# A three-layer graph network on one core: banks for the search of places, the place of its preparation, and the pacing of the first layer's seam

## The chip, the core and the metric

One of the eight cores of a Trainium2 chip runs the whole program. The metric is the device time of one execution in microseconds (us); the kernel before takes 2237.45 us, the median of three runs (2230.03 to 2240.05). The engines named below are PE (TensorE matmuls; PEld is its load of weights), DVE (VectorE), ACT (ScalarE), POOL (GpSimd) and SP (SyncE, used here only to issue transfers). PSUM is the memory that PE sums into; it has 8 banks of 512 fp32 per partition.

## The reference

A graph of 6,250 nodes and 100,000 edges, sorted by the node that they end in, goes through three layers. A layer multiplies the node rows by a weight matrix, adds the rows of the neighbours (with loops, both ends scaled by 1/sqrt(degree)), adds a bias and takes the positive part. The result is added to the input, and each row is normalised.

```python
loops = jnp.arange(n); src = concat([src, loops]); dst = concat([dst, loops])
deg = segment_sum(ones, dst, n); dinv = rsqrt(deg)
norm_edge = dinv[src] * dinv[dst]
h = x                                   # 6250 x 256
for W, b in ((W1, b1), (W2, b2), (W3, b3)):   # 256x512, 512x512, 512x256
    h = relu(segment_sum((h @ W)[src] * norm_edge[:, None], dst, n) + b)
x = layernorm(x + h)                    # rows of 256, eps 1e-5
```

## The kernel before

**Tiling.** Nodes are cut into 50 blocks of 125 (Q), degrees and loads into groups of 10 blocks (GRP). The sums over edges of a block are formed in one of two ways. A *gathered* block fetches the rows of its edges from a table in DRAM: POOL issues one indirect transfer of 128 rows at a time (L1365 in the first layer, L1561 in the others), and PE adds the rows to their nodes by a matmul with a one-hot matrix that DVE makes by comparing (L1321). A *dense* block multiplies a 125 by 6,250 matrix of edge counts with all node rows, which lie in SBUF in `parts` (L1450): 50 matmuls, one for each block of sources. These count matrices are themselves made in the first layer by `counts`: DVE compares (L1032) make one-hot matrices, PE multiplies them (L1105), ACT copies the counts out as uint8 (L1066), and SP stores them to `kept` in DRAM.

**Stages.** The *opening* loads the edges (L766, on the queues of SP, ACT and POOL), makes constants (`numbers`, `finder_numbers`), and runs five groups of degree stages (`counted`, from L829): counts of edges per node, 1/sqrt(degree), scaled rows to the first table, and at the end the node rows split into `parts` (`in_parts`, L891 on ACT and L892 on DVE). Then the *first layer* runs (`first_layer`, L1274): 466 gathers for blocks 21 to 49, while blocks 0 to 20 (FEW) are dense. The *second layer* (`layer(1, ...)`) has 599 gathers of 512-wide rows, the *third* (`layer(2, ...)`) 317 gathers and 32 dense blocks with `after3`, which ends in the normalised rows.

**What sets the order.** The whole program is recorded in one fixed order by generators that hand over to each other (`manual_schedule`): the layer's loop takes one gather after another, and with each gather every helper takes a step or counts down its pause (`yield 3` is three gathers). Each engine executes its own instructions strictly in the order recorded. So a number in a helper moves instructions of all engines against each other. The helpers that matter here:

- The **search of places** (`found_rounds` L588, `found_beyond` L628, called by `all_found` L674) works out for 34 blocks, two at a time, which edges the second and third layers gather in which round; its results are `round_src` and `over_src`. It sums into `spot[0]`, which in the first layer is the upper half of the bank `near` (L1008). The lower 250 columns of `near` hold the numbered columns that every DVE compare of L1032 and L1321 reads; a profile's tile name `near_cols` is this bank. `rows_risen` (L567) prepares the search; it runs in the opening's loop, once per group from group 10 on (L932 to L935), summing into `mat_bank`.
- **Banks.** Seven banks circulate in a queue, `common`. A dense sum, a gathered sum, a pair of counts each take one (`one_of_common`) and put it back. `counts` takes one only while more than SPARE stay behind.
- **`teams`** (L1138): four groups of four blocks of the second layer are dense, 800 steps of two matmuls (L1195) over the first layer's result, into four fixed banks. They can start when all counts are stored, the search is done and the result's first rows are back in `parts`. `first_layer` runs some of these steps at its end, the second layer FRONT of them (L1607) before its first product, and `team_goal` (L1899) spreads the rest evenly so that they end TEAMS_END gathers before the last gather.
- **`caching`** (L1123): when all 21 dense blocks of the first layer have ended, SP loads the first layer's result from its table into `parts`, two blocks every three gathers.
- Blocks 26 to TAIL_FROM-1 of the first layer gather 2 KB rows that are already split into two parts; blocks from TAIL_FROM on gather 1 KB rows, which ACT (L1417) and DVE (L1420) split.

Of the kernel before, what the change touches and what calls it, by code (L numbers as in the profile page):

```python
# [23 lines left out]
P = 128  # L24
# [19 lines left out]
SPARE = 1  # L44
# [7 lines left out]
TAIL_FROM = 47  # L52
# [3 lines left out]
FRONT = 24  # L56
TEAMS_END = 70
# [345 lines left out]
def sorted_path(ctx: ExitStack, tc: tile.TileContext, x, edges, starts, found, wts, biases, room, late, out):  # L403
# [105 lines left out]
    spot = [mat_bank[:, :256]]  # L509
    finder_room = room[:, room.shape[1] - 4 * C - 584:room.shape[1] - 4 * C]  # L510
    out_of = finder_room[:, :CHOSEN * WAYS].rearrange("p (c w) -> p c w", w=WAYS)
    hit, value = [finder_room[:, 252 + n * CHOSEN * KF:][:, :CHOSEN * KF].rearrange("p (c j) -> p c j", j=KF) for n in range(2)]
    run = finder_room[:Q, 476:476 + 4 * KF].rearrange("p (b j) -> p b j", b=2)
# [53 lines left out]
    def rows_risen(g, ed, spare):  # L567

        b0 = max(g, FIRST_EDGES)
        size = g + GRP - b0  # L570
        of = slice(b0 - FIRST_EDGES, g + GRP - FIRST_EDGES)
        bits = spare[:, :size * KF].bitcast(BF16).rearrange("p (b k j) -> p b k j", k=2, j=KF)
        for k in range(2):
            number = spare[:, (k + 1) * 2 * P:][:, :size * KF].bitcast(I32).rearrange("p (b j) -> p b j", j=KF)
            nc.vector.tensor_single_scalar(number, ed[:, b0:g + GRP, :, 0], (6, 63)[k], op=(ALU.logical_shift_right, ALU.bitwise_and)[k])
            nc.scalar.copy(bits[:, :, k], number)
        yield
        half = -(-size // 2)
        for n in range(2):
            for b, e in ((0, half), (half, size)):  # L580
                risen = spot[0][:, :(e - b) * 2 * KF]
                nc.tensor.matmul(risen, lhsT=row_steps[n], rhs=bits[:, b:e].rearrange("p b k j -> p (b k j)"), start=True, stop=True)
                yield
                for k in range(2):
                    nc.scalar.activation(rises[:, of, k, 1 + n * KF:1 + (n + 1) * KF][:, b:e],
                                         risen.rearrange("p (b k j) -> p b k j", k=2, j=KF)[:, :, k], AF.Copy, scale=0.5)

    def found_rounds(e):  # L588

        two, bank = range(e, e + 2), spot[0]  # L590
# [7 lines left out]
        yield  # L598
# [5 lines left out]
        yield  # L604
        got = finder.tile([Q, 2, 2, 2 * KF + 1], F32, name="egot")
        nc.scalar.copy(got.rearrange("p b k j -> p (b k j)"), bank[:Q, :2 * each])
        yield
# [18 lines left out]
        yield  # L626

    def found_beyond(e):  # L628

        two, bank = range(e, e + 2), spot[0]  # L630
# [3 lines left out]
        yield  # L634
        for n, m in zip(two, marks):
            for at in (slice(0, 2 * P), slice(2 * P, LANES)):
                wide = at.stop - at.start
                nc.tensor.matmul(bank[:, :wide], lhsT=low_of[:, n, 0:1].to_broadcast([P, P]), rhs=m[:, at], start=True, stop=True)  # L638
                yield
                nc.scalar.activation(past[:, n - e, at], bank[:, :wide], AF.Sign, bias=less16)  # L640
                yield
# [11 lines left out]
        yield  # L653
        nc.scalar.copy(out_of, ways)
        yield
# [14 lines left out]
        yield  # L670
# [3 lines left out]
    def all_found():  # L674

        ahead = 1
# [76 lines left out]
    with tc.tile_pool(name="sdeg1", bufs=1) as dp1, tc.tile_pool(name="sdeg", bufs=2) as dp, \  # L753
# [3 lines left out]
        row_steps = [dp1.tile([P, P], BF16, name=f"esteps{n}") for n in range(2)]  # L757
# [136 lines left out]
        with tc.manual_schedule():  # L894
# [7 lines left out]
            numbers()  # L902
            load_edges(POOL, nc.gpsimd, range(8, GRP))
# [10 lines left out]
            steps_of_numbers = finder_numbers(find_space)  # L914
# [11 lines left out]
            for k in range(NG + 2):  # L926
# [20 lines left out]
            for g in range(2 * GRP, NB, GRP):  # L947
                in_parts(g)
# [174 lines left out]
    def caching():  # L1123

        while finished < FEW:
            yield 1
# [989 lines left out]
```

## Time and profile before

| what | us |
|---|---|
| median of three runs (lowest, highest) | 2237.45 (2230.03, 2240.05) |
| the profiled execution, whole | 2235.24 |
| its span, from first to last instruction | 2233.4 |
| first gather issued | 102.7 |

A profile shows one execution. "Busy" is the time in which an engine executes; a row of groups gives the line, the engine, output and input tiles, the count, the busy time with the mean ns of one, then the engine's idle time just before these instructions and what ended most of it. A row of waits reads: engine, tile and line that waited, then the engine, tile and line waited for, and the total us, the number of waits, the longest. A row of windows gives the busy time of every engine in a stretch with its number of instructions, the granted TensorE clock (1.00 is full), the mean busy share of the 16 DMA engines (over 1 where rows overlap) and GB/s.

### The profile page before, as it was taken

What the parts mean: (1) busy time and instruction counts of PE and PEld (TensorE: products, weight loads), DVE (VectorE), ACT (ScalarE), POOL (GpSimd) and SP (SyncE); (2) the same over time, 40 slices, a digit from 0 to 9 for tenths busy, and PEclk for the clock granted to TensorE, in tenths of its full rate; (3) what the DMA queues carried; (4) which work ended last, traced back from release to release, by engine and by line L of the source; (5) the groups of instructions that cost most, each with busy time, mean ns of one, the idle gap of its engine ahead of it and who ended that gap; (6) DMA issues with size and microseconds to landing.
All of it is one profiled execution on the core that took longest, in us unless ns stands there. A gap on an engine that the chain in (4) does not pass through costs nothing. (4 is left out here: it accounts for less than half of the span.)

```text
span 2233.4 us, 29538 instructions
## 1 busy us (share of the span) xinstructions
PE 1887.6 (85%) x8654; PEld 1433.4 (64%) x8654; DVE 1583.6 (71%) x3141; ACT 1121.3 (50%) x2183; POOL 1434.9 (64%) x1426
## 2 busy tenths in 40 slices
PE   2468988788889965968999899899976889999996
PEld 1356666555666633646787687688765666777775
DVE  5576677677767773577777777767767468888876
ACT  0546566566667643633444444445433345555552
POOL 2145555455557655577777777777776477777775
PEclk9989999999999966979999999999988899999998
DMA  6566477677679999477777777777788567777784
GB/s 145 156 200 191 134 202 179 169 184 189 180 201 256 250 300 233 137 235 208 218 221 224 210 220 222 213 217 220 217 244 227 152 172 202 201 203 206 204 213 128
DMA packets 227394, 451.33 MB, mean 202 GB/s; under 512 B 44147, under 2 KB 103234, under 8 KB 227220
## 3 DMA queue, kind: packets, MB, share of 16 engines
q0 software_dynamic: 119376, 305.25, 50.1%
q1 hardware_dynamic: 92004, 132.23, 21.3%
q10 hardware_dynamic: 15840, 11.86, 2.1%
q8 instruction: 70, 1.15, 0.2%
q14 instruction: 104, 0.85, 0.1%
HBM read 376.81 MB, written 69.81 MB: 200 GB/s over the span
## 5 line engine op out<-in xcount | busy, mean ns | idle before, releaser
L1561 POOL DMA_INDIRECT room<-tab,round_src x728 | 765.8, 1052 | 265.9 <-issue 132.8
L1621 DVE TENSOR_TENSOR total<-total,room 125x512 f32<-125x512 f32 (+1 forms) x694 | 410.6, 592 | 82.8 <-DMA room<-tab,round_src 72.0
L1365 POOL DMA_INDIRECT halves<-both,efirst_src x318 | 300.5, 945 | 240.7 <-PE sacc L1399 59.6
L1032 DVE TENSOR_TENSOR room<-near_cols,slots 128x625 bf16<-128x625 f32 (+2 forms) x390 | 300.2, 806 | 119.8 <-PE near_cols L638 31.9
L1162 ACT CAST dense_rows<-parts 125x512 fp32r<-125x512 f32 x200 | 123.9, 619 | 270.6 <-PE smm L1195 268.6
L1164 DVE TENSOR_TENSOR dense_rows<-parts,dense_rows 125x512 fp32r<-125x512 f32 x200 | 137.9, 689 | 133.8 <-ACT dense_rows L1162 131.5
L1561 POOL DMA_INDIRECT room<-tab,over_src x182 | 189.0, 1038 | 64.5 <-issue 34.1
L1271 ACT CAST piece<-room 125x625 fp32r<-125x625 uint8 x217 | 151.8, 713 | 106.3 <-PE win_ps L1644 35.1
L1365 POOL DMA_INDIRECT room<-tab,efirst_src x128 | 128.4, 1003 | 102.6 <-PE smm L1399 31.0
L1577 PE MATMUL sacc<-halves,shot 128*125 128x512 f32 x430 | 144.3, 437 | 51.4 <-ACT halves L1613 36.5
L1195 PE MATMUL sacc<-dense_rows 125*125 125x512 f32 x400 | 140.9, 427 | 43.1 <-DVE dense_rows L1164 16.8
L1613 ACT CAST halves<-room 128x512 fp32r<-128x512 f32 (+1 forms) x188 | 101.0, 544 | 148.6 <-DMA room<-tab,over_src 87.4
L1616 DVE TENSOR_TENSOR halves<-room,halves 128x512 fp32r<-128x512 f32 (+1 forms) x188 | 110.6, 598 | 62.7 <-ACT halves L1613 60.3
L1271 ACT CAST dense_rows<-room 125x625 fp32r<-125x625 uint8 x210 | 149.3, 724 | 6.6 <-PE smm L1450 1.9
L1105 PEld LDWEIGHTS <-room 128*125 128x125 bf16 x650 | 90.1, 147 | 87.3 <-issue 65.0
L1577 PEld LDWEIGHTS sacc<-halves,shot 128*125 128x125 f32 x430 | 86.5, 203 | 87.0 <-ACT halves L1613 41.9
L1644 PE MATMUL win_ps<-parts,piece 125*125 125x512 f32 x550 | 139.5, 405 | 0.0
L1195 PE MATMUL mat_ps<-dense_rows 125*125 125x512 f32 x400 | 136.4, 423 | 0.5 <-DVE room L1740 0.5
L1195 PE MATMUL smm<-dense_rows 125*125 125x512 f32 x400 | 135.2, 419 | 1.1 <-DVE room L1740 1.1
L1644 PE MATMUL smm<-parts,piece 125*125 125x512 f32 x505 | 128.4, 407 | 8.1 <-DVE piece L1271 8.1
L1195 PE MATMUL near_cols<-dense_rows 125*125 125x512 f32 x400 | 133.8, 416 | 0.0
L1321 DVE TENSOR_TENSOR shot<-near_cols,edlo 128x500 fp32r<-128x500 f32 x110 | 74.0, 673 | 77.5 <-PE sacc L1399 29.4
(460 smaller groups left out, 4326.5 us busy)
## 6 DMA issues: line engine op xcount, KB each, us to landing
kept<-room SPq DMA_DIRECT2D x32, 683.6 KB
room<-kept SPq DMA_DIRECT2D x32, 683.6 KB
tab<-st SPq DMA_DIRECT2D x58, 224.0 KB
parts<-tab SPq DMA_DIRECT2D x28, 448.0 KB
room<-tab,round_src POOLq DMA_INDIRECT x728, 3.9
both<-parts SPq DMA_DIRECT2D x10, 1120.0 KB
room<-kept SPq DMA_DIRECT2D x160, 68.4 KB
room<-in_x SPq DMA_DIRECT2D x50, 112.0 KB
```

What stands on the lines that cost most here:

```text
L1032: nc.vector.tensor_tensor(out, numbered[0][:, :shape[2]].unsqueeze(1).to_broadcast(shape), numbers.unsqueeze(2).to_broadcast(shape), op=AL ...
L1162: nc.scalar.copy(to[:, :HID], row)
L1164: nc.vector.tensor_sub(to[:, HID:], row, to[:, :HID].bitcast(F32))
L1195: nc.tensor.matmul(team_banks[n][:Q], lhsT=team_pieces[u % 2][:, n, :], rhs=both_parts[u % 2][:, h * HID:(h + 1) * HID], start=(u % NB == ...
L1271: convert(piece, matrix[:, c * PIECE:(c + 1) * PIECE, :])
L1365: nc.gpsimd.indirect_dma_start(out=row, out_offset=None, in_=table, in_offset=bass.IndirectOffsetOnAxis(ap=at, axis=0))
L1561: nc.gpsimd.indirect_dma_start(out=row, out_offset=None, in_=tables[i], in_offset=bass.IndirectOffsetOnAxis(ap=at, axis=0))
L1577: nc.tensor.matmul(acc[:Q, :size], lhsT=hots[b][:, k], rhs=two[:, c0:c0 + size], start=(k == c0 == 0), stop=(k == BEYOND + 1 and c0 + size ...
L1613: nc.scalar.copy(two[:, :width], landed[chunk - hi_lag])
L1616: nc.vector.tensor_sub(two[:, width:], landed.pop(chunk - lo_lag), two[:, :width].bitcast(F32))
L1621: nc.vector.tensor_add(own, parts[:, b].bitcast(F32) if i == 1 and r == 0 else own, landed.pop(chunk - ADDED[i])[:Q])
L1644: nc.tensor.matmul(acc_d[:Q], lhsT=got[done // PIECE][:, k % PIECE, :], rhs=parts[:, k], start=(k == 0), stop=(k == NB - 1))
```

## The change

Three things change.

1. The search of places takes a bank from `common` for each piece of its work and gives it back, in place of the half of `near`; `counts` may take the last bank (SPARE 0). The two matmuls of `found_beyond` per block, 256 and 192 columns wide, become one of 448, and so do the two ACT signs behind them. Since banks are no longer in known places, `teams` collects three of `common` beside `near`, and the later layers take what is left.
2. `rows_risen` leaves the opening's loop. Its bits are made once at the opening's end, behind `in_parts` (`bits_of`), and its matmuls, 6 in place of 16, stand at the head of `all_found`, in the first layer. The two POOL iotas of `finder_numbers` are issued ahead of POOL's edge loads in place of behind them.
3. At the seam to the second layer `caching` begins when the last dense block of the first layer is still being summed, following its matmuls (`dense_done`), and pauses four gathers in place of three. TAIL_FROM goes from 47 to 46. FRONT goes from 24 to 12, the first 18 gathers (HEAD) bring two team steps each, and TEAMS_END goes from 70 to 36.

```diff
-SPARE = 1
+SPARE = 0
-TAIL_FROM = 47
+TAIL_FROM = 46
-FRONT = 24
-TEAMS_END = 70
+FRONT = 12
+TEAMS_END = 36
+HEAD = 18
...
     def finder_numbers(spare):
         part_i = spare[:, 0:1].bitcast(I32)
+        lane_i = spare[:, P:P + LANES].bitcast(I32)
         nc.gpsimd.iota(part_i, pattern=[[0, 1]], base=0, channel_multiplier=1)
-        lane_i = spare[:, P:P + LANES].bitcast(I32)
         nc.gpsimd.iota(lane_i, pattern=[[1, LANES]], base=0, channel_multiplier=0)
         yield
...
+    def bits_of(ed, spare):
+        number = [...]
+        for h in range(2):
+            of = slice(h * NE // 2, (h + 1) * NE // 2)
+            for k in range(2):
+                nc.vector.tensor_single_scalar(number[k], ed[:, FIRST_EDGES:, :, 0][:, of], (6, 63)[k],
+                                               op=(ALU.logical_shift_right, ALU.bitwise_and)[k])
+                nc.scalar.copy(bits[:, of, k], number[k])
+
+    def rows_risen():
         for n in range(2):
-            for b, e in ((0, half), (half, size)):
-                risen = spot[0][:, :(e - b) * 2 * KF]
-                nc.tensor.matmul(risen, lhsT=row_steps[n], rhs=bits[:, b:e]..., start=True, stop=True)
-                yield
+            for b in range(0, NE, 16):
+                of = slice(b, min(NE, b + 16))
+                bank = yield from one_of_common(0)
+                risen = bank[:, :(of.stop - b) * 2 * KF]
+                nc.tensor.matmul(risen, lhsT=row_steps[n], rhs=bits[:, of]..., start=True, stop=True)
+                yield 1
                 for k in range(2):
                     nc.scalar.activation(...)
+                common.append(bank)
+                yield 1
...
     def found_rounds(e):
-        two, bank = range(e, e + 2), spot[0]
+        two = range(e, e + 2)
+        bank = yield from one_of_common(0)
...
     def found_beyond(e):
+        bank = yield from one_of_common(0)
         for n, m in zip(two, marks):
-            for at in (slice(0, 2 * P), slice(2 * P, LANES)):
-                wide = at.stop - at.start
-                nc.tensor.matmul(bank[:, :wide], lhsT=low_of[:, n, 0:1].to_broadcast([P, P]), rhs=m[:, at], ...)
-                yield
-                nc.scalar.activation(past[:, n - e, at], bank[:, :wide], AF.Sign, bias=less16)
-                yield
+            nc.tensor.matmul(bank[:, :LANES], lhsT=low_of[:, n, 0:1].to_broadcast([P, P]), rhs=m, ...)
+            yield 1
+            nc.scalar.activation(past[:, n - e], bank[:, :LANES], AF.Sign, bias=less16)
+            yield 1
...
     def all_found():
+        yield from rows_risen()
...
             load_edges(ACT, nc.scalar, [g + b for g in later for b in range(4, 8)])
             numbers()
+            steps_of_numbers = finder_numbers(find_space)
+            next(steps_of_numbers)
             load_edges(POOL, nc.gpsimd, range(8, GRP))
...
-                g = (k - 2) * GRP
-                if FIRST_EDGES // GRP * GRP <= g < NB:
-                    for _ in rows_risen(g, ed, find_space):
-                        pass
...
             for g in range(2 * GRP, NB, GRP):
                 in_parts(g)
+            bits_of(ed, find_space)
             late_w()
...
-    team_banks = [accs[2], mat_bank, near, mm_bank]
+    team_banks = []
     common += accs + [mm_bank, tr_bank, mat_bank]
-    spot[0] = near[:, 256:]
+    all_banks = [*common, near]
...
     def caching():
-        while finished < FEW:
+        while finished < FEW - 1:
             yield 1
         for k in range(0, NB, 2):
-            while not {k, k + 1} <= rows_made:
+            while finished < FEW and (k >= FEW - 2 or dense_done < (FEW - 1) * NB + k + 2) or not {k, k + 1} <= rows_made:
                 yield 1
...
-                yield 3
+                yield 4
...
     def team_goal(chunk, total):
         most = NB * TEAM * TEAMS
-        goal = min(most, steps_before + (chunk + 1) * (most - steps_before) // (total - TEAMS_END))
+        head = steps_before + FRONT + 2 * min(chunk + 1, HEAD)
+        goal = min(most, head + max(0, chunk + 1 - HEAD) * (most - head) // (total - TEAMS_END - HEAD))
```

How the order recorded stands before and now is shown at three places; L numbers are those of each kernel's own file (the new file's are some lines higher).

POOL in the opening, before: the end of its edge loads, then the two iotas (`w_58` is the space that `finder_numbers` works in), the search's first transfer and the first gather.

```order
L763 TENSOR_LOAD starts
L766 ISA
L766 DMA ed<-in_edges 128x32
L519 IOTA w_58 128x1
L521 IOTA w_58 128x448
L720 DMA w_sb<-in_edges,w_sb 125x256
L1365 DMA room<-tab_170,rest 128x256
```

POOL now: the same iotas stand ahead of the first edge load.

```order
L801 MEMSET seps 128x1
L802 MEMSET szero 1x512
L522 IOTA w_58 128x1
L523 IOTA w_58 128x448
L771 TENSOR_LOAD starts
L774 ISA
L774 DMA ed<-in_edges 128x32
```

ACT in the opening, before: the degree stage of the last group but one, with the casts and copies of `rows_risen` (L576, L585) inside it.

```order
L868 COPY ends<-sdeg_ps 125x10
L871 CAST ecount<-sdeg_ps 125x10
L873 COPY over_lo<-edlo 128x10
L576 CAST w_58<-w_58 128x10x16 x2
L585 ACTIVATE erises<-mat_ps 128x5x16 x8
L877 COPY eends<-sdeg_ps 125x10
L883 ACTIVATE room<-room,sdinv 125x256 x5
```

ACT now: the same stage without them.

```order
L876 COPY ends<-sdeg_ps 125x10
L879 CAST ecount<-sdeg_ps 125x10
L881 COPY over_lo<-edlo 128x10
L885 COPY eends<-sdeg_ps 125x10
L891 ACTIVATE room<-room,sdinv 125x256 x5
```

PE in the first layer, before: a matmul of `found_beyond` between a gathered product and a pair of counts, into the bank of the numbered columns.

```order
L1450 MATMUL sacc_1043<-parts,dense_rows 125x512 x3
L1399 MATMUL win_ps<-room,shot 125x256
L638 LDWEIGHTS elow
L638 MATMUL near_cols<-emarks_200,elow 128x256
L1105 LDWEIGHTS room
L1105 MATMUL str<-room 125x250
```

PE now: one matmul of 448 columns, into a bank from the queue (here `win_ps`).

```order
L1453 MATMUL sacc_986<-parts,dense_rows 125x512 x3
L1402 MATMUL sacc_985<-room,shot 125x256
L645 LDWEIGHTS elow
L645 MATMUL win_ps<-emarks_200,elow 128x448
L1111 LDWEIGHTS room
L1111 MATMUL mat_ps<-room 125x250
```

SP at the seam, before: the first two loads back into `parts` stand behind two blocks' rows (`tab_171`) and two count matrices (`kept`).

```order
L80 DMA kept<-room 112x6250
L80 DMA kept<-room 13x6250
L82 DMA parts<-tab_171 112x2x512
L82 DMA parts<-tab_171 13x2x512
L82 DMA parts<-tab_171 112x2x512
L82 DMA parts<-tab_171 13x2x512
L80 DMA tab_171<-st 112x512
L80 DMA tab_171<-st 13x512
```

SP now: the first load stands ahead of a count matrix that it stood behind, and it is recorded 18 gathers earlier (355 in place of 373).

```order
L81 DMA tab_171<-st 112x512
L81 DMA tab_171<-st 13x512
L83 DMA parts<-tab_171 112x2x512
L83 DMA parts<-tab_171 13x2x512
L81 DMA kept<-room 112x6250
L81 DMA kept<-room 13x6250
L83 DMA parts<-tab_171 112x2x512
L83 DMA parts<-tab_171 13x2x512
```

Counted in the same recorded order: `found_beyond` issues 34 PE matmuls and 34 ACT operations fewer, `rows_risen` 6 matmuls in place of 16 and 12 ACT activations in place of 32 (with 4 casts in place of 8); the tail from block 46 adds 16 gathers of 1 KB with 16 splits on ACT and on DVE, and takes 16 gathers of 2 KB away; there are 1,383 gathers in both. The search ends at gather 308 of the first layer in place of 290, the team steps done before the second layer's loop are 98 in place of 69, at its gather 24 they are 154 in place of 103, and they end at its gather 563 in place of 529. A bank that is given back and taken again within the same gather occurs 263 times in 375 uses, in place of 63 in 329, from gather 10 to 290 of the first layer.

More of the change, by code (lines that the diff above doesn't have):

```diff
@@ L1168, in teams @@
         numbered[0] = cols
-        for bank in team_banks:
-            while bank is not near and not any(one is bank for one in common):
-                yield 1
-            for _ in range(len(common)):
-                one = common.popleft()
-                if one is not bank:
-                    common.append(one)
+        while len(team_banks) < TEAM - 1:
+            team_banks.append((yield from one_of_common(0)))
+        team_banks.append(near)
         fetch_counts(0)
@@ L1470, in layer @@
         idle.clear()
-        idle.update(acc=accs[:2] if i == 1 else list(accs), acc_d=[mm_bank, win_bank, mat_bank])
+        if i == 1:
+            idle.update(acc=[common.popleft() for _ in range(2)])
+            wins.extend(common)
+        else:
+            banks = [bank for bank in all_banks if bank is not team_banks[0]]
+            idle.update(acc=banks[:3], acc_d=[team_banks[0], *banks[3:5]])
+            spare_banks.extend(banks[5:])
         items = []
```

61 lines of the change are left out of this document (27 added, 34 removed).

## Prediction, made before the changed kernel ran

> **What bounds the kernel now.** The views were read in this order: the page's totals, the windows by stage, the waits of the binding engine in each stage, then single instructions. The page first:
>
> ```profile
> span 2233.4 us, 29538 instructions
> PE 1887.6 (85%) x8654; PEld 1433.4 (64%) x8654; DVE 1583.6 (71%) x3141; ACT 1121.3 (50%) x2183; POOL 1434.9 (64%) x1426
> L1561 POOL DMA_INDIRECT room<-tab,round_src x728 | 765.8, 1052 | 265.9 <-issue 132.8
> ```
>
> PE has the largest share, but 85% is a mean over stages. The windows below are the opening, the first layer's body, the end of its counts, the seam to the second layer, the start and body of the second layer, its end, and the third layer:
>
> ```profile
> core 0: us, PE busy (x) PEld busy (x) DVE busy (x) ACT busy (x) POOL busy (x), PEclk, DMA share, GB/s
> 0.00:103.00 103.00, 36.44 (x221) 28.32 (x221) 56.90 (x195) 33.06 (x107) 15.61 (x38) 1.00 0.60 147
> 126.00:655.00 529.00, 450.81 (x2418) 323.22 (x2417) 366.44 (x784) 320.78 (x651) 273.10 (x287) 0.97 0.66 179
> 655.00:740.00 85.00, 82.53 (x390) 60.26 (x389) 67.03 (x113) 62.82 (x113) 59.42 (x64) 1.00 0.90 243
> 740.00:926.00 186.00, 138.75 (x484) 86.86 (x484) 111.92 (x194) 92.50 (x184) 110.93 (x114) 0.79 0.96 246
> 945.00:1675.00 730.00, 661.67 (x2877) 529.47 (x2875) 528.61 (x819) 333.39 (x623) 563.33 (x536) 0.96 0.76 221
> 1675.00:1790.00 115.00, 84.32 (x365) 67.71 (x365) 66.14 (x105) 39.96 (x78) 63.84 (x62) 0.85 0.67 187
> ```
>
> Four kinds of stretch. In the opening no engine is busy for more than 57 of 103 us: a chain sets it. From 126 to 655 PE is busy 451 of 529 us, and no other engine reaches 70%: PE's 78 us of idle time are the reserve. From 655 to 740 PE is full. From 740 to 926 the DMA engines are (share 0.96), and PE idles 47 us. In the second layer's body POOL issues 536 gathers in 730 us, 1.36 us each: 1.05 busy (563/536) and 0.31 in its own issue gap, as its waits say (122.8 us in 402 waits):
>
> ```profile
> POOL room L1561 <- issue: 122.8, 402, 0.5
> POOL room L1561 <- DVE total L1621: 8.8, 21, 1.5
> ```
>
> Other releasers hold POOL there for single rows below 13 us, so gathers pace it, though PE with 662 of 730 is close behind.
>
> PE's waits from 126 to 655, longest first; the eight rows of `near_cols` sum to 57.0 us, and the three on L1066, where a bank of counts waits for its copy by ACT, to 5.8 in 13 waits:
>
> ```profile
> PE near_cols L638 <- DVE room L1032: 23.1, 17, 3.6
> PE near_cols L593 <- DVE room L1032: 7.5, 6, 1.8
> PE near_cols L593 <- DVE shot L1321: 6.8, 4, 3.3
> PE near_cols L638 <- DVE emarks L633: 5.9, 3, 2.9
> ...
> PE near_cols L602 <- DVE room L1032: 4.8, 7, 1.1
> PE near_cols L638 <- DVE shot L1321: 3.5, 2, 2.0
> PE near_cols L650 <- DVE room L1032: 3.1, 4, 1.5
> PE sacc L1105 <- ACT room L1066: 2.7, 7, 0.7
> PE near_cols L602 <- DVE shot L1321: 2.3, 2, 1.3
> PE smm L1105 <- ACT room L1066: 1.9, 3, 1.5
> ...
> PE sacc L1695 <- ACT room L1066: 1.2, 3, 0.7
> ```
>
> So the search's matmuls wait until DVE has finished a compare that only reads the other half of the same bank, and all of PE's queue stands behind them.
>
> **The opening: -14 us.** Its rows:
>
> ```profile
> 30.70 0.52 POOL L521 IOTA w<- 128x448 int32 x1
> 31.25 0.39 DVE L523 CAST elanes<-w 128x448 f16<-128x448 int32 x1 [14.51 <-POOL w L521]
> L766 ACTq DMA_DIRECT2D ed<-in_edges x20: 339/340/383, 14.4 to 44.1; - x20
> 51.00 0.18 ACT L866 ACTIVATE sroot<-sdeg_ps 125x10 f32<-125x10 f32 x1 [37.06 <-PE sdeg_ps L858]
> 93.23 0.54 ACT L576 CAST w<-w 128x160 bf16<-128x160 int32 x2
> 96.39 0.37 ACT L585 ACTIVATE erises<-mat_ps 128x80 bf16<-128x80 f32 x2 [0.38 <-PE mat_ps L582]
> 97.23 4.55 ACT L891 CAST parts<-room 125x2560 fp32r<-125x2560 f32 x2
> 102.70 3.31 POOL L1365 DMA_INDIRECT room<-tab,rest  x1 [19.77 <-DVE parts L892]
> ```
>
> DVE stands still for 14.5 us until POOL, done with its edge loads, makes the iotas. With these ahead, DVE's constants and the first degree stage come up to 14.5 us earlier. ACT's first degree operation (L866) came at 51.0, but ACT issues loads until 44.1 + 0.3 = 44.4: of the 14.5 at most 51.0 - 44.4 = 6.6 reach ACT's chain. That is my value. The two iotas delay POOL's edge loads by about the 0.6 us they take, which lies under the other queues' loads. Second, `rows_risen`: the last group's part runs from 93.23 to 96.76, 3.5 us on ACT straight ahead of L891, which releases the first gather. The three earlier parts cost ACT as much, but the next stage's ACT work waits for DVE anyway, so I count one of them as on the path, 3.5. Together 7, and 6.6: -14. What `bits_of` adds (4 DVE and 4 ACT operations, nearest row L576, 0.27 us per 160 columns, so about 0.46 per 272 and under 2 us on ACT) stands behind the last `in_parts`, hence behind the first gather's release. Bounds: -7 (only one of the two terms arrives) to -22 (14.5 + 7).
>
> **The search: -39 us.** With a bank of its own no matmul of the search waits for compares of the columns: -57 if nothing takes the place. Something does. The search now takes banks from the same queue as the counts and sums, and the counts may take the last one. By the recorded order 200 more uses begin with a bank given back within the same gather (263 in place of 63), so their first matmul waits for the reader that empties it. Before, 63 such uses cost 5.8 us, 0.09 each; 200 cost 18. The other bound is a whole reader each:
>
> ```profile
> L1066 ACT CAST room<-sacc 125x500 uint8<-125x500 f32 (+1 forms) x106 | 71.8, 687 | 1.5 <-PE sacc L1105 1.3
> ```
>
> 200 x 0.69 = 138 us, that is +81 net. I take 0.09, as it was measured on the same kind of use, and ACT is busy 321 of 529 us, so it mostly reads soon. Bounds -57 to +81, of which the positive end is the rival below.
>
> **Work that moves: +2.** The 34 halves of L638 that fall away leave the same columns to multiply; ACT saves 34 operations, where it has 208 us free. `rows_risen` brings 6 matmuls of up to 512 columns into the PE-bound stretch, at 0.4 each (the 512-wide step below is 0.46): +2. Its 12 ACT operations lie in ACT's free time. Bounds 0 to +5.
>
> **The seam: -8 us.** Rows of 740 to 926 and just behind it:
>
> ```profile
> PE sacc L1195 <- ACT dense_rows L1162: 12.1, 1, 12.1
> PE mat_ps L1399 <- DMA halves<-both,efirst_src: 10.1, 10, 1.5
> PE smm L1399 <- DMA halves<-both,efirst_src: 9.8, 13, 1.6
> POOL room L1561 <- DMA parts<-st: 16.8, 1, 16.8
> 885.61 0.63 PE L1195 MATMUL near_cols<-dense_rows 125*125 125x512 f32 x2
> 886.07 0.62 PE L1195 MATMUL smm<-dense_rows 125*125 125x512 f32 x2
> ```
>
> The DMA engines are full here, so a load that starts earlier only moves into a stretch with room if there is one, and 655 to 740 is already at 0.90. What is truly less is one block's gathers at 1 KB in place of 2 KB: 16 x 128 x 1 KB = 2.1 MB, at the window's 246 GB/s 8.5 us. The 16 more splits fall to ACT and DVE, busy 93 and 112 of 186. `caching`'s loads now wait on SP for dense matmuls recorded two steps ahead; behind them on SP stand stores of rows and count matrices, and the team work waits for these stores. Since PE is at most a few steps behind its order, I count that as nothing. The 29 team steps that move ahead of the second layer cost PE 0.46 each (885.61 to 886.07), 13 us, against 47 idle. Bounds: 0 (the loads' new order costs what the bytes give) to -30 (also the 12.1 and 16.8 us waits at the loads go).
>
> **The second layer: 0, its end +2.** From its gather 24 to 529 it now holds 92 fewer steps (51 done before, 41 left behind). POOL's pace, 1.36 us per gather, does not depend on them as long as gathers bind. At the end 41 steps x 0.46 = 19 us of PE work shift into the last 70 gathers and the window to 1790, where PE is busy 84 of 115 and waits for loads of the third layer:
>
> ```profile
> POOL room L1561 <- DMA tab<-st: 23.2, 1, 23.2
> POOL room L1561 <- DVE total L1621: 11.9, 8, 2.9
> ```
>
> The later blocks' `after2` rows feed the table that the 23.2 us wait is for, so a little is late: +2, bounds -10 to +10.
>
> **The sum.** -14 - 39 + 2 - 8 + 0 + 2 = -57. Against the profiled execution, 2235.24 us whole, that is 2178.2; the median of the runs shown is 2.2 above it: **2180 us**.
>
> **Rivals.**
>
> *The second layer follows PE.* If its PE, 91% busy, paces the gathers through its waits for sums, 92 steps x 0.46 = 42 us more go: 2180 - 42 = 2138. Against it: POOL's 1.36 per gather is complete from its own two numbers.
>
> *Another thing holds the first layer.* The waits on `near_cols` are long since DVE's compares come late; if DVE (366 of 529) and the gathers hold the stage, PE's 57 us of idle time come back under other names, the +18 with them. Left are -14, -8 and the two +2: 2235.24 - 18 + 2.2 = about 2219. For it: the waits' releaser is DVE throughout, which the counts need too.
>
> *Banks run dry (slower).* In the first layer, `counts` takes the last bank, and each of 200 reuses waits for ACT's whole copy, 0.69 us: 138 - 57 = +81, with the rest's -18: 2237.45 + 63 = about 2300. It decides from (57 + 14 + 8 - 4) / 200 = 0.38 us per reuse, four times what such uses cost now. For it: ACT executes in order, and its copies queue behind splits and scalings.
>
> *No change.* The chip's granted clock can eat the gain: it is 0.97 in the first layer's body, 1.00 in the full stretch behind it, 0.79 in the seam, where PE is busy 75%. If the body fell to 0.79, its 451 us would be 451 x 0.97 / 0.79 = 554, above the 529 it has now: +25, with the same -18: about 2244. The Trainium skill, page "TensorE: Matmul & The Clock Gate", section "A second HAM failure mode: psum-queue depth-cycling", describes matmul groups that cycle through PSUM's banks and idle so briefly and often that the clock swings between half and full, which is the manner of this change. The trace agrees only for the seam's 0.79, where the waits are for transfers; the first layer already cycles seven banks at 0.97.
>
> **How the numbers follow.** Forecast 0.60, the second layer on PE 0.08, first layer held otherwise 0.16, banks dry 0.10, no change 0.06. The forecast's own range is 2154 (no cost of reuse: -18, opening -22: -8) to 2217 (opening -7, seam 0, 0.2 us per reuse: +7, +8, +22). The whole range goes from 2135 (the PE rival) to 2232, which takes in the held case and reuses of 0.35 us (2180 + 200 x 0.26), and leaves out the dry and the unchanged case, 0.16, and a little below. Half a per cent is about what a measurement of this kernel tells from no change, 11 us: faster means below 2226. That holds for forecast, PE rival and held case but a tail (0.82); within 2226 to 2249 is the unchanged case and that tail (0.07); above lie the dry case and a worse clock (0.11).
>
> **What would show it.** In the changed profile no wait of PE in the search names DVE's compares, DVE's 14.5 us gap is gone, and the first gather comes at about 89. PE's busy share from there to the search's end is above 0.9, and waits on the counts' copy sum to under 25 us. The second layer's body still takes 1.36 us per gather with fewer PE instructions in it. Wrong would be: the first layer's body as long as now with new names on PE's waits; copy waits above 75 us; a first gather at 95 or later; a granted clock below 0.9 in that body; or a second layer whose gathers come faster than now.

## The result and the profile after

The changed kernel takes 2178.09 us (median of four runs, 2175.28 to 2186.77) against 2236.23 for the kernel before beside it (four runs): a ratio of 0.9749, 95% interval 0.9712 to 0.9787, or 58 us less. A later set on a chip that runs the kernel before in 2232.2 gave 2170.51 and 0.9730 (0.9679 to 0.9780). The page of the changed kernel, its first two lines:

```profile
span 2178.6 us, 29385 instructions
PE 1877.0 (86%) x8610; PEld 1429.2 (66%) x8610; DVE 1584.5 (73%) x3148; ACT 1120.9 (51%) x2138; POOL 1437.7 (66%) x1426
```

The windows that answer to those before, for the first layer's body, its seam, the second layer's body and its end (columns as there):

```profile
111.00:593.00 482.00, 445.42 (x2415) 323.56 (x2415) 372.26 (x798) 325.95 (x630) 275.70 (x290) 0.98 0.74 204
...
676.50:860.00 183.50, 139.64 (x522) 94.37 (x521) 115.81 (x206) 98.63 (x204) 115.92 (x117) 0.85 0.92 238
...
883.00:1613.00 730.00, 646.78 (x2743) 508.70 (x2741) 517.92 (x801) 316.09 (x591) 564.08 (x536) 0.96 0.75 217
1613.00:1737.00 124.00, 95.76 (x436) 78.52 (x436) 72.71 (x109) 48.75 (x89) 61.21 (x63) 0.90 0.73 197
```

In the first layer's body PE does nearly the same work (2,415 matmuls, 445 us) in 482 us in place of 529. The second layer's body is what it was: 536 gathers in 730 us, with 134 PE matmuls fewer in it. Gathers stand in the same order in both programs, so the start of a gather divides the time cleanly. The table has the time of each stretch from the starts of POOL's gathers (each layer's counted from 0), for the trace before and two traces of the changed kernel:

| stretch | before | changed | changed, later set | forecast of the difference |
|---|---|---|---|---|
| start to first gather | 102.7 | 87.9 | 87.2 | -14 |
| first gather to gather 350 | 633.6 | 588.5 | 584.4 | -37 (search -39, moved work +2) |
| gather 350 to 466 (seam) | 185.4 | 183.1 | 183.0 | -8 |
| 466 to the second layer's gather 529 | 739.0 | 739.7 | 730.7 | 0 |
| its gather 529 to the third layer | 127.0 | 135.2 | 139.9 | +2 |
| third layer, to the end | 445.8 | 444.2 | 442.9 | 0 |
| span | 2233.4 | 2178.6 | 2168.1 | -57 |

The first layer up to gather 350 is the stretch that counts. PE's idle time there (length less PE's busy time in a window of it) was 633.6 - 538.0 = 95.6 us; it is 588.5 - 533.0 = 55.5 now. The waits of PE in that stretch, changed kernel, longest first:

```profile
PE sacc L586 <- ACT room L577: 9.6, 2, 9.4
PE sacc L1402 <- DMA room<-tab,efirst_src: 6.9, 2, 5.0
PE win_ps L1705 <- DVE st L1710: 4.9, 3, 3.3
PE sacc L1673 <- DVE st L1710: 4.1, 2, 2.8
...
PE win_ps L1111 <- ACT room L1072: 2.8, 2, 2.5
PE sacc L1111 <- ACT room L1072: 2.6, 5, 1.4
PE mat_ps L1111 <- ACT room L1072: 2.5, 4, 1.6
```

No row of `near_cols` is left; in the stretch before, such rows summed to 77.8 us, 70.1 of them on compares (the forecast's 57.0 were those of 126 to 655; the rest lay ahead of 126 and behind 655). The waits on the counts' copies (L1072, L1066 before) sum to 8.3 us now and to 8.0 before, though uses of a bank within the same gather rose from 63 to 263. New are 10.0 us more on `st` (11.8 for 1.8: banks that DVE reads in `after1`), 9.6 us at the very start where PE waits for the moved bits, and 10.2 us for gathered rows that have not landed.

ACT shows why the copies come so promptly. Its waits in the first layer to gather 350, before:

```profile
ACT epast L640 <- DVE shot L1321: 47.5, 20, 5.2
ACT epast L640 <- DVE room L1032: 46.1, 21, 5.3
...
ACT epast L640 <- PE near_cols L638: 15.1, 7, 4.1
...
ACT ereached L597 <- DVE room L1032: 14.2, 6, 4.3
ACT room L654 <- DVE room L1032: 12.8, 7, 4.8
```

And the same view of the changed kernel, its rows of the search's signs:

```profile
ACT epast L647 <- PE sacc L645: 8.6, 8, 2.8
ACT epast L647 <- PE win_ps L645: 8.2, 5, 3.2
...
ACT epast L647 <- PE mat_ps L645: 7.0, 6, 1.6
```

Before, ACT too stood behind the compares with the signs that it took from the shared bank, 93.6 us in 41 waits at `epast` alone (its third row, 15.1, is a wait for PE's own matmul), and the counts' copies stood behind it in its queue. Now no sign waits for a compare: `epast` waits for PE's matmuls only, 29 us in all.

The opening, changed kernel: ACT's first degree operation and its first scaling, and the first gather:

```profile
47.78 0.18 ACT L874 ACTIVATE sroot<-sdeg_ps 125x10 f32<-125x10 f32 x1 [33.12 <-DMA ed<-in_edges]
48.30 4.09 ACT L891 ACTIVATE room<-room,sdinv 125x256 f32<-125x256 f32 x10 [0.33 <-DVE sdinv L883]
```

```profile
87.94 3.31 POOL L1368 DMA_INDIRECT room<-tab,rest  x1 [13.15 <-DVE parts L900]
```

ACT's issue of edge loads (the last eight from 32.81 for 14.86 us) still holds the first degree operation, as the forecast had it, though until 47.8 (51.0 before). But behind it the scaling waits 0.33 us for DVE in place of 3.18, since DVE is a stage ahead, and the next group's first operation comes without the 1.74 us that it waited for PE. By the second group's scaling ACT is 7.9 us ahead (56.87 for 64.80).

### The profile page after: what moved, and what is told of

It is laid out like the page before. It is cut to its first block, busy times and chain, and to the rows that moved or that the text cites. A ratio compares the mean times of both kernels' runs of the same rounds, so it can differ in the third digit from the quotient of the medians.

```text
span 2178.6 us, 29385 instructions
## 1 busy us (share of the span) xinstructions
PE 1877.0 (86%) x8610; PEld 1429.2 (66%) x8610; DVE 1584.5 (73%) x3148; ACT 1120.9 (51%) x2138; POOL 1437.7 (66%) x1426
## 4 chain that ended last, share of the span: by engine, by line
PE 43%; DMA 21%; DVE 13%; issue 9%; POOL 6%; ACT 4%; SPq 0%; ACTq 0%; POOLq 0%; DVEq 0%
DMA room<-tab,round_src 10%; POOL room L1571 6%; PE smm L1654 5%; PE sacc L1453 4%; DMA room<-tab,over_src 4%; PE sacc L1654 4%; PE str L1654 4%; DVE room L1038 4%; DMA room<-tab,efirst_src 2%; PE sacc L1402 2%; DMA halves<-both,efirst_src 2%; DVE total L1631 2%; PE smm L1789 2%; PE sacc L1587 1%; PE sacc L1705 1%
## 5 line engine op out<-in xcount | busy, mean ns | idle before, releaser
L1571 POOL DMA_INDIRECT room<-tab,round_src x728 | 762.4, 1047 | 280.1 <-issue 138.6
L1368 POOL DMA_INDIRECT halves<-both,efirst_src x304 | 286.9, 944 | 194.9 <-PE sacc L1402 51.9
L1038 DVE TENSOR_TENSOR room<-near_cols,slots 128x625 bf16<-128x625 f32 (+2 forms) x390 | 295.0, 802 | 28.0 <-PE sacc L1111 13.3
L1368 POOL DMA_INDIRECT room<-tab,efirst_src x144 | 146.4, 1017 | 103.5 <-PE sacc L1402 28.8
L1197 PE MATMUL sacc<-dense_rows 125*125 125x512 f32 x400 | 146.7, 441 | 60.6 <-DVE dense_rows L1170 25.9
L1453 PE MATMUL sacc<-parts,dense_rows 125*125 125x512 f32 x600 | 192.7, 428 | 2.7 <-ACT dense_rows L1274 2.5
L1654 PE MATMUL smm<-parts,piece 125*125 125x512 f32 x550 | 141.7, 410 | 0.0
L1111 PEld LDWEIGHTS <-room 128*125 128x125 bf16 x650 | 89.3, 144 | 77.8 <-issue 47.4
L1197 PE MATMUL win_ps<-dense_rows 125*125 125x512 f32 x400 | 138.3, 428 | 1.5 <-DVE room L1750 1.5
L1654 PE MATMUL sacc<-parts,piece 125*125 125x512 f32 x505 | 127.6, 405 | 8.9 <-DVE piece L1274 8.9
L1197 PEld LDWEIGHTS sacc<-dense_rows 125*125 125x125 f32 x400 | 73.9, 191 | 91.5 <-DVE dense_rows L1170 35.8
```

What stands on the lines that cost most here:

```text
L1038: nc.vector.tensor_tensor(out, numbered[0][:, :shape[2]].unsqueeze(1).to_broadcast(shape), numbers.unsqueeze(2).to_broadcast(shape), op=AL ...
L1197: nc.tensor.matmul(team_banks[n][:Q], lhsT=team_pieces[u % 2][:, n, :], rhs=both_parts[u % 2][:, h * HID:(h + 1) * HID], start=(u % NB == ...
L1368: nc.gpsimd.indirect_dma_start(out=row, out_offset=None, in_=table, in_offset=bass.IndirectOffsetOnAxis(ap=at, axis=0))
L1453: nc.tensor.matmul(acc_d[:Q], lhsT=got[done // PIECE][:, k % PIECE, :], rhs=parts[:, k], start=(k == 0), stop=(k == NB - 1))
L1571: nc.gpsimd.indirect_dma_start(out=row, out_offset=None, in_=tables[i], in_offset=bass.IndirectOffsetOnAxis(ap=at, axis=0))
L1654: nc.tensor.matmul(acc_d[:Q], lhsT=got[done // PIECE][:, k % PIECE, :], rhs=parts[:, k], start=(k == 0), stop=(k == NB - 1))
```

## The experiments

Twelve runs, of nine kernels, make four sets. A set's runs share one chip and are measured against the kernel before on it. In three sets the kernel before took 2470 to 2501 us in place of 2232: those chips run the same program slower, most of all in the second layer (below). So a ratio counts within its set, and stretches are compared only between chips of one kind.

**The search back in the half bank (first and third set).** All else as changed, SPARE 0 included.

```diff
-        bank = yield from one_of_common(0)
+        bank = spot[0]                    # near[:, 256:]
...
-            nc.tensor.matmul(bank[:, :LANES], ..., rhs=m, ...)
+            for at in (slice(0, 2 * P), slice(2 * P, LANES)):
+                nc.tensor.matmul(bank[:, :wide], ..., rhs=m[:, at], ...)
```

> The changed kernel with the search of places put back into the upper half of the bank of numbered columns, and its 448 columns back in two matmuls; all else as changed. Theory (the wait on the shared bank was the cost): PE's waits on near_cols come back with 55 to 80 us in the search, the stretch from the first gather to gather 350 grows from 588.6 us by 35 to 50, and the whole is 2215 to 2228. Rival (the first layer is held by DVE and the gathers anyway, the gain came from the counts' last bank and from the opening): below 2195, with the waits on near_cols below 25 us.

> The search back in the upper half of the bank of numbered columns, as in the first job, for a chip on which the kernel before takes about 2232 to 2237 (the changed kernel there: 2170 to 2178). Theory (the wait on the shared bank costs 57 to 78, less what the reuse of banks gives back): 2210 to 2225, first gather to gather 350 some 625 to 640 in place of 584 to 588, waits of PE on near_cols above 55. Rival (the stretch is held by DVE and the gathers): below 2190.

Measured: 2501.06 and 2502.04, ratios 1.0018 (0.9990 to 1.0045) and 1.0011 (0.9988 to 1.0034), on the slower kind of chip. First gather to gather 350 takes 680.7 and 684.0 us; the kernel with the old seam, whose program up to there is the changed one's, takes 612.3 and 607.1 in the same two sets. With the half bank, and the narrower matmuls that come back with it, the stretch is 68 to 77 us longer, more than the 35 to 50 expected. The first gather comes at 85.9 and 86.8 us, as early as in the changed kernel, and yet the whole takes as long as the kernel before. Where the other edits lose on this kind of chip what the opening gains isn't shown, as the kernel before left no trace there. Windows of that stretch, third set, first this kernel, then the one with the old seam:

```profile
86.80:770.80 684.00, 557.69 (x2863) 397.51 (x2863) 465.13 (x939) 401.19 (x796) 344.56 (x356) 0.95 0.65 178
```

```profile
86.70:693.80 607.10, 539.76 (x2834) 389.12 (x2834) 455.13 (x938) 397.77 (x761) 345.18 (x357) 0.98 0.73 201
```

PE idles 126.3 us with the shared bank and 67.3 without (127.6 and 67.4 in the first set), so 59 of the 77 us are waiting; the rest is busy time of PE, 557.7 us for 539.8. The waits of PE with the shared bank:

```profile
PE near_cols L647 <- DVE shot L1326: 15.4, 9, 4.0
PE sacc L1113 <- ACT room L1074: 13.5, 12, 2.1
PE near_cols L647 <- DVE room L1040: 13.4, 8, 2.7
...
PE smm L1113 <- ACT room L1074: 7.7, 5, 2.6
...
PE win_ps L1113 <- ACT room L1074: 5.6, 7, 1.6
```

Those on compares that read `near_cols` sum to 39 us (all rows of `near_cols` to 50), not the 55 expected, and those on the counts' copies (L1074) to 34.0 in 31 waits. ACT stands behind the compares again:

```profile
ACT epast L649 <- DVE room L1040: 52.7, 28, 4.0
ACT epast L649 <- DVE shot L1326: 19.8, 8, 3.9
```

This kernel has 162 uses of a bank within the same gather. With ACT held, an extra use costs an estimated (34.0 - 8.0) / (162 - 63) = 0.26 us, taking the 8.0 of the kernel before on the first chip. The kernel with the old seam, on the same chip as this one, has 263 such uses, as the changed kernel has, and its waits on these copies are 8.0 us in 15. So most of the price of reuse comes with the shared bank: it is dear where ACT is held, and the bank holds ACT.

**A bank for the search alone; SPARE back at 1 (first set, the second also in the third).** Six banks for counts and sums, with SPARE 1, in the first; only SPARE changed in the second.

```diff
-    common += accs + [mm_bank, tr_bank, mat_bank]
+    common += accs + [mm_bank, mat_bank]
+    spot[0] = tr_bank                     # back to common when the search ends
```

```diff
-SPARE = 0
+SPARE = 1
```

> The changed kernel with one bank kept for the search alone until it ends, so that the counts and sums share six and one stays behind as before the change (SPARE 1). Theory (what matters is that the search doesn't share the bank of the columns, and banks used again at once cost little): 2170 to 2192, no waits on near_cols in the search. Rival (supply of banks sets the stage; a bank used again at once costs 0.38 us or more): above 2205, with waits of PE on the counts' copies above 40 us.

> The changed kernel with SPARE back at 1, so that the counts leave one bank behind. Theory (uses of a bank at once after it is given back cost 0.05 us or less): 2172 to 2186. Rival (they cost what the prediction summed, 18 us or more, and SPARE 0 makes most of them): 2160 or less. Second rival (counts starve and the search's end moves the counts back): above 2192.

> SPARE back at 1, which leaves 70 uses of a bank given back within the same gather, of 338, in place of 263 of 375 (gathers 10 to 290). Theory (such a use costs 0.05 us or less): within 8 us of the changed kernel, first gather to gather 350 within 578 to 594. Rival (0.09 as summed): that stretch 17 us shorter, 568 to 571. Second rival (a bank in hand is needed): 600 or more.

Measured: the own bank 2393.88, ratio 0.9585 (0.9548 to 0.9622); SPARE 1 2386.56 and 2397.90, ratios 0.9567 (0.9525 to 0.9608) and 0.9571 (0.9538 to 0.9604). The absolute figures expected don't apply on this chip. A private bank is no better than one from the queue, so it is the sharing with the columns that cost. Stretch to gather 350 with SPARE 1, third set:

```profile
86.50:666.40 579.90, 512.85 (x2667) 369.71 (x2666) 425.08 (x896) 364.60 (x704) 343.80 (x356) 0.96 0.75 205
```

It is 27 us shorter than the 607.1 above, as the rival with dear reuse would have it; but it holds 167 matmuls fewer, since the counts lag, and PE idles 579.9 - 512.9 = 67.0 us against 67.3 (72.5 and 67.4 in the first set). With 70 uses within the same gather PE waits as long as with 263. The shorter stretch is work put off, not waiting saved. But the work put off isn't paid for at the seam: gather 350 to 466 takes 185.8 and 188.8 us with SPARE 1, 199.2 and 198.9 with the old seam and SPARE 0, and PE idles 46.3 us there in place of 60.0 (third set). From the first gather to gather 466 SPARE 1 is 37 to 42 us ahead (768.7 us for 806.0 in the third set, where the stack kernel, with the new seam, takes 812.8). So on this kind of chip SPARE 0, a part of the change, seems to cost time, though not by reuse. On a chip where the kernel before takes 2232 us, SPARE 1 did not run.

**Banks as a stack (third set).** The bank given back last is taken first.

```diff
-        return common.popleft()
+        return common.pop()
```

> The changed kernel with the queue of banks turned into a stack: the bank given back last is taken first, 303 uses of 375 within the same gather in place of 263, and those whose bank was given back by the counts' copy 205 in place of 153. Theory (0.05 or less): within 5 us of the changed kernel. Rival (0.38 to 0.69 us each, the price from which the slower case decided): 15 to 28 us slower.

Measured: 2439.71, ratio 0.9743 (0.9708 to 0.9778); the changed kernel has no run on this kind of chip. Against the kernel with the old seam, the same to gather 350 but for the banks, PE idles 613.0 - 539.3 = 73.7 us for 67.3, with waits on copies of 15.4 in 24 for 8.0 in 15: 7.4 us for 52 more uses behind a copy, 0.14 each. A use costs about that when the queue is made to seek it: more than the 0.05 expected, and far below the 0.38 from which the slower case decided.

**The whole seam undone (first and third set).**

```diff
-TAIL_FROM = 46
+TAIL_FROM = 47
...
-        while finished < FEW - 1:
+        while finished < FEW:
...
-        head = steps_before + FRONT + 2 * min(chunk + 1, HEAD)
-        goal = ...
+        goal = min(most, steps_before + (chunk + 1) * (most - steps_before) // (total - TEAMS_END))
```

> The changed kernel with the whole third part undone: loads back into parts as before, TAIL_FROM 47, FRONT 24, even spread of the team steps to 70 gathers before the end. The prediction's terms: seam +8, end of the second layer -2, so 2184. Reading of the traces after: seam +2, end -8.5, so about 2172. Rival (the seam's part is worth its whole byte sum and the end is not its work): 2186 or more, with the second layer's last gather still 109 us behind its gather 529.

> The third part undone, as in the first job, for this chip. The prediction's terms: gather 350 to 466 8 us longer, the end of the second layer 2 shorter: 6 slower than the changed kernel. Reading of the traces: gather 350 to 466 2 longer, gather 529 to the third layer 8 to 12 shorter: 6 to 10 faster than the changed kernel in that sum, though the second layer's body may give 9 back as it did with TEAMS_END 70.

Measured: 2420.25 and 2417.50, ratios 0.9700 (0.9661 to 0.9739) and 0.9655 (0.9618 to 0.9691). Gather 529 to 598 of the second layer takes 111.9 and 114.4 us, where kernels with the new pacing take 120.9 to 127.0 in these sets: the end of the second layer is lost to the pacing. Gather 350 to 466 takes 199 us against 199.8 in the stack kernel, which has the new seam and SPARE 0 (194.0 and 197.2 with the half bank): on this chip the seam's edits move little or nothing there. What its parts are worth one by one wasn't tried.

**The changed kernel again, TEAMS_END 70, the iotas put back (second set, kernel before 2232.2).**

```diff
-TEAMS_END = 36
+TEAMS_END = 70
```

```diff
             numbers()
-            steps_of_numbers = finder_numbers(find_space)
-            next(steps_of_numbers)
             load_edges(POOL, nc.gpsimd, range(8, GRP))
...
             idle_slots = 0
+            steps_of_numbers = finder_numbers(find_space)
```

> The changed kernel itself, as the measure for the others of this job and for the ones before it, whose kernel before took 2498 in place of 2237. If the job's kernel before is again near 2498: theory (banks used again at once cost 0.05 us or less) gives the changed kernel within 10 us of the one with SPARE 1, which was 111 below the kernel before; rival (0.15 us each for the 193 that SPARE 1 saves, as the first layer of the kernel with the old seam hints) gives 80 below. If it is near 2237: about 2178 again.

> The changed kernel with TEAMS_END back at 70, so that the team steps end 34 gathers earlier; nothing else. Theory (the end of the second layer lost 8 us because the last team sums, their rows and the loads behind them come later): 6 to 10 us below the changed kernel, and from gather 529 to the third layer's first gather about as before the change. Rival (that stretch is lost to the chip's clock or the transfers): within 3 us of the changed kernel. Second rival (the denser team steps slow the second layer's gathers): 5 us or more above it.

> The changed kernel with the two iotas back behind POOL's edge loads, rows_risen still moved. The prediction's term: the first gather 6.6 us later than in the changed kernel, and DVE's gap of 14 us back. Rival (ACT's issue of the edge loads sets the first degree stage anyway, as the trace after shows it until 47.7): 0 to 3.5 us later.

Measured: the changed kernel 2170.51, ratio 0.9730 (0.9679 to 0.9780); TEAMS_END 70 2165.39, ratio 0.9700 (0.9667 to 0.9732); the iotas put back 2179.23, one run. With TEAMS_END 70, gather 529 to the third layer takes 130.4 us, 9.5 less than the changed kernel in the same set. POOL's waits from 1600 to 1790 before, and from 1540 to 1737 in the changed kernel (later set) and with TEAMS_END 70, each to just behind the third layer's first gather:

```profile
POOL room L1561 <- DVE total L1621: 13.8, 12, 2.9
```

```profile
POOL room L1571 <- DVE total L1631: 27.1, 14, 6.7
```

```profile
POOL room L1571 <- DVE total L1631: 12.4, 11, 4.0
```

A gather there waits for DVE to add the row that lies in its place; DVE does so between its work for the team steps and for the last sums' rows. With the steps ended earlier these waits are as short as before. But the second layer's body then takes 689.0 us from gather 24 to 529, against 679.2, so of the 9.5 nothing is sure: the two medians differ by 5.1 us within overlapping intervals.

With the iotas put back the first gather comes at 96.7 us, against 87.2 and 85.6 in this set, and DVE's gap is there again:

```profile
32.08 0.39 DVE L525 CAST elanes<-w 128x448 f16<-128x448 int32 x1 [14.27 <-POOL w L523]
```

So between these traces the iotas are worth 9.5 to 11 us and `rows_risen` the remaining 102.7 - 96.7 = 6.0. In the result's own pair of traces the split is 7.9 (above) and 14.8 - 7.9 = 6.9.

**SPARE 1 and TEAMS_END 70 together (fourth set).**

> The changed kernel with SPARE 1 (70 uses within the same gather in place of 263) and TEAMS_END 70. Where the kernel before takes about 2235, the changed kernel took 2170 and 2178 and the one with TEAMS_END 70 alone 2165. Theory (a use costs 0.05 or less, and what counts lose in banks they make up by gather 466): 2158 to 2172. Rival (0.09 as summed, 193 uses): 2150 or less. Second rival (the counts come later and the team steps with them): above 2175. Where the kernel before takes about 2500, the kernels with SPARE 1 took 2387 and 2398: theory 2378 to 2398.

Measured: 2355.10, kernel before 2470.15, ratio 0.9540 (0.9509 to 0.9570), the lowest ratio of all. The chip is again of the slower kind, where the changed kernel itself never ran; that this version beats it is not shown. The two ratios of SPARE 1 alone are above it and their intervals overlap with it. Gather 529 to 598 of the second layer takes 114.3 us, as with the whole old seam and 7 to 13 less than with the new pacing, so TEAMS_END seems to give the end back on this kind of chip too.

## Why the prediction came out, step by step

The time forecast was 2180, the time measured 2178. The steps that carry it hold, but four terms were off and cancelled: the search gave 8 to 12 us more than forecast, the seam 6 less, and the second layer's end lost 6 to 11 more. That the total lies within 2 us is luck.

**The opening: right in size, off in its parts.** -14 was forecast, -14.8 and -15.5 measured. "Of the 14.5 at most 6.6 reach ACT's chain" failed: the iotas brought 7.9 in the result's pair of traces and 9.5 to 11 in the later set. ACT's first operation came only 3.2 us earlier, but DVE's head start was kept in the stages behind it (0.33 us of waiting in place of 3.18). `rows_risen` brought 6.0 to 6.9 for the 7 forecast.

**The search: mechanism right, size too small.** -37 with the moved work was forecast, -45.1 and -49.2 measured. The wait on the shared bank is shown twice: its rows vanish from the changed kernel, and with the half bank restored PE idles 59 us more. The -57 was too small, since its window left out 20.8 us of the same rows. The term that failed is the +18 for banks used again at once. Its rule, 0.09 us for each of 200 uses on the counts' copies, came out as +0.3, with +10.0 on banks that DVE reads for `st`; only 153 of the 263 uses are of a bank that a counts' copy gave back. The 0.09 had been measured while ACT itself stood behind the compares; the same edit that makes reuse frequent takes away what made the reader late. So the slower rival, whose price was 0.38, never came near: an estimated 0.26 per use with the shared bank kept, 0.14 with the stack, and none that can be seen with the queue.

The Trainium skill, page "PSUM — Partial Sum Buffer", section "PSUM bank collisions raise a hardware error", says that engines must be kept apart by bank and quadrant and not by address, disjoint columns and two readers included. The trace before agrees in that the program keeps them apart so: PE waited 23.1 us in 17 waits, and ACT 46.1 in 21, for compares that read other columns of the bank.

**The rival that the first layer is held otherwise** came partly true: of the 77.8 us of waits some 37 came back under other names (98.1 us of named waits in the stretch before, 57.5 now), not all of them.

**The clock.** The granted clock in the first layer's body is 0.98 (0.97 before), with banks cycled faster than ever. The Trainium skill, page "TensorE: Matmul & The Clock Gate", section "A second HAM failure mode: psum-queue depth-cycling", describes matmul groups that cycle through PSUM's banks and idle so often that the clock swings between half and full. No trace here bears it out: from the first gather to gather 350 the mean granted clock is 0.95 to 0.99 in all of them, 0.97 in the kernel before.

**The seam: too large.** -8 was forecast from bytes, -2.3 and -2.4 measured. The DMA share fell from 0.96 to 0.92, and 246 GB/s over 186.0 us against 238 over 183.5 is 2.1 MB less, so the bytes did go. But the waits at the loads stayed (10.7 and 17.2 us for 12.1 and 16.8), and POOL took over some of the wait. Its rows at the seam, before and now:

```profile
POOL room L1365 <- DVE halves L1420: 5.5, 10, 2.7
```

```profile
POOL room L1368 <- DVE halves L1423: 14.5, 13, 7.6
```

A 1 KB row is free only when ACT and DVE have split it. The forecast counted the 16 more splits as hidden by DVE's free time; what counted was when they were done. That this is the whole of the missing 6 us is argued, not shown.

**The second layer: right; its end: too small.** The body keeps 1.36 us per gather with 134 matmuls fewer (+0.7 and -8.3 against 0 over its stretch, about the spread between traces). The end lost 8.2 and 12.9 where +2 was taken, one within and one beyond the bound of 10: the 23.2 us wait for the table was the wrong row to look at, the gathers' waits for DVE's additions the right one.

## What to carry to other kernels

A PSUM bank that is read all the time by one engine should hold nothing else: two engines stood behind its readers here, and where banks were also reused at once, PE's waits for copies by the second, held as it was, came to 34 us in place of 8. A price measured per event holds only while its cause stays; ask whether the edit also removes what made the event dear. When a helper's steps are spread to the end of a loop, look at which in-order engine must serve both them and the loop's last rows.

## What was not expected of the hardware

In three of four sets the chip ran the kernel before 11 to 12% slower, and not evenly: the second layer's gathers 24 to 529 took 793 to 817 us for 679 to 689, while the first 350 gathers of the changed program took 607 to 612 for 584 to 588. The granted clock in that part of the second layer is lower too, 0.89 to 0.93 for 0.95 to 0.97, but most of the time is lost idle. The kernel with the half bank, whose program there is the changed one's, keeps PE busy 648.1 of 810.5 us (first set), the changed kernel 612.3 of 679.3 (later set): 95 of the 131 us more are idle time. The slower traces show engines that wait for nothing the profile names, for example ACT from 950 to 1700 us with SPARE 1 and TEAMS_END 70:

```profile
ACT dense_rows L1168 <- remote: 99.4, 21, 9.5
ACT dense_rows L1168 <- issue: 65.2, 27, 5.4
```

The changed kernel's trace in the result has no such rows there. The mean time of one of the 728 gathers by `round_src` on POOL is the same (1034 ns with SPARE 1 in the first set, 1047 in the changed kernel), so it isn't the issue of gathers itself. The cause stays open. It means that a gain measured on one of these chips need not have that size on another.
